# A planned graph-and-experts kernel whose list scheduler gets a finer model, searches its order by small changes, and makes weight loads wait for gathered rows

## The chip, the cores and the metric

The kernel runs on one core of a Trainium2 chip. The metric is device time in microseconds of one execution. A profiled execution gives a trace beside it; its span (first to last recorded instruction) is a little shorter than the time of the same execution. Engines are called by the profile's names: PE (TensorE matmuls), PEld (weight loads of TensorE), DVE (VectorE), ACT (ScalarE), POOL (GpSimd), SP (SyncE, which here issues DMAs). Each engine works off its own queue in order and waits for others by semaphores.

## The reference

Input x has 3327 rows of 256 numbers, the adjacency is 3327 by 3327 of zeros and ones with ones on the diagonal. Two layers follow one another, each with a layernorm ahead and a residual around it:

```
def gnn(x, adj, W, a, gamma, beta):                # H = 4 heads of D = 64
    h = (x @ W).reshape(n, H, D)
    s = einsum('nhd,d->nh', h, a[:D, 0] + a[D:, 0])
    e_row = leaky_relu(s, 0.2)
    e = where(adj[:, None, :] > 0, e_row[:, :, None], -9e15)   # same score for all neighbours of a row
    h_prime = einsum('nhm,mhd->nhd', softmax(e, -1), h).reshape(n, H * D)
    return layernorm(h_prime) * gamma + beta

def ffn(x, gate_w, gate_b, w1, w2, w3):            # 16 experts, 256 -> 512 -> 256
    probs = softmax(x @ gate_w + gate_b)
    top_probs, top_idx = top_k(probs, 2)           # the two weights are divided by their sum
    hidden = silu(x @ w1[e]) * (x @ w2[e])
    return sum over the two experts of weight * (hidden @ w3[e])

x = x + gnn(layernorm(x), adj, ...)
x = x + ffn(layernorm(x), ...)
```

Since a row's score is the same for all its neighbours, the softmax weights of a row are equal, and the aggregation is a product of the zero-one adjacency with h.

## The kernel before

**Stages.** Rows are padded to 3328 = 26 tiles of 128 and cut into seven groups of 4, 4, 4, 4, 3, 4 and 3 tiles. The *h stage* takes a group's rows: statistics on DVE (L503, L504), transposes and the product with W on PE (L484, L492), then a split of the result into a high part (ACT, L495) and a low part (DVE, L498, called lo). Column sums of W that make the scores are worked out ahead of it (L462 to L472). The *aggregation* has 7 x 7 = 49 steps, one for a pair of groups: SP loads a block of the transposed adjacency (L572, sg), DVE converts it (L575, mk), and PE multiplies it with the high and the low part (L598, L599), 676 times each. A *group's end* follows its last step: DVE and POOL make the normalised rows (L653 to L706; square roots on POOL, L435 to L438), PE transposes the result x1 (L722), ACT copies it, and PE makes the gate's logits (L730) and turns them back (L739). DVE finds the two best experts, PE works out each row's place in its expert's list (L784 to L788, L823), ACT writes normed rows (L716), and SP stores them to `normed` in DRAM (L839) and x1 to the output (L614).

**Expert lists.** There are 19 lists of rows. Lists 0 to 2 hold the rows of experts 0 to 2 from the first five groups, lists 3 to 5 the rest of these experts, lists 6 to 18 the other thirteen experts. For a list POOL gathers rows of `normed` by an indirect DMA (L970), one for every 128 rows; DVE picks the row's weight out of the gathered row ("weigh", L976 and L978, which so waits for the DMA); the rows are transposed, for lists below 8 on PE (L1174, ACT copy L1183), from 8 on by DMA transposes of their 16-bit halves (L1137, L1138, L1128). Lists below 6 use plain up products (L985), a silu on ACT (L1198) and a product on DVE (L1201). Lists from 6 on use a scheme with seven products for eight (`by_sevenths`: sums of weights and rows on DVE at L1018, products L1046, copies on ACT L1052 and adds on DVE L1056, silu L1078, product L1081). Down products are L1099 (L1095 for a part of a tile). The result is scaled by the row's weight on ACT (L1222) or DVE (L1224) into the tile y, and POOL adds its rows into the output by an indirect DMA (L1102). SP loads an expert's three weight blocks (L330 to L332) into w12e and w3e; for lists from 6 on it reads the expert's number from a table first.

**What sets the order.** No queue is written by hand. Every piece of work is entered with `plan.add(engine, cost, rank, after, emit, uses, landing, size, slack, step)`. `uses` names buffers with a number of slots each (six for y, three for gathered rows, four for accumulators of the aggregation). `order` is a list scheduler: among all works whose predecessors are placed it takes the one that can start earliest, ties by rank, with a little luck added to works of rank 3. `start_of` works out that earliest start: the engine's free time, predecessors' ends plus HOP (nothing for a predecessor on the same engine), and the freeing of a slot. `place` books it; a DMA with a size goes through one line with a rate, in order of issue. `run` makes 80 orders from 80 seeds, replays each six times with up to 10% noise on the costs of engines other than PE, and emits the instructions in the order with the least total. So every engine's queue is the order of emission, and all costs are only numbers for the planner; an instruction waits for what it really depends on.

Of the kernel before, what the change touches and what calls it, by code (L numbers as in the profile page):

```python
# [37 lines left out]

# [13 lines left out]
ALU = mybir.AluOpType  # L52
# [7 lines left out]
H = 4  # L60
# [55 lines left out]
class Plan:  # L116
# [3 lines left out]
    HOP = 0.2  # L120
    RATE = 380e3
    ORDERS, LUCK = 80, 0.2
    REPLAYS, SPREAD = 6, 0.1
# [13 lines left out]
    def restart(self):  # L137
        for work in self.works:
            work.end = None
        self.free = {work.engine: 0.0 for work in self.works}  # L140
        self.taken, self.held, self.line = {name: [] for name in self.slots}, set(), 0.0

    def start_of(self, work, slack):

        at = self.free[work.engine]
        for w in work.after:
            if w.end is None:
                return None
            at = max(at, w.end + (0 if w.engine == work.engine and not w.landing else self.HOP + slack))
# [11 lines left out]
    def place(self, work, at, cost):  # L161
# [4 lines left out]
        self.free[work.engine] = work.end = at + cost  # L166
# [6 lines left out]
    def order(self, seed):  # L173

        draw = random.Random(seed).random
        luck = {work: draw() * self.LUCK if seed and not callable(work.rank) and work.rank[0] == 3 else 0.0 for work in self.works}
        self.restart()
        todo, order, step = list(self.works), [], -1
        while todo:
            best = None  # L180
            for work in todo:
                at = self.start_of(work, work.slack)
                if at is not None:
                    rank = work.rank(step) if callable(work.rank) else work.rank
                    if best is None or (at + luck[work], rank) < best[:2]:
                        best = (at + luck[work], rank, at, work)
            if best is None:
                return None
            _, _, at, work = best
            todo.remove(work)  # L190
            order.append(work)
            self.place(work, at, work.cost)
            step = step if work.step is None else work.step
# [10 lines left out]

    def run(self):
        orders = [order for order in map(self.order, range(self.ORDERS)) if order]
        order = min(orders, key=lambda o: sum(self.replay(o, seed) for seed in range(1, self.REPLAYS + 1)))
# [11 lines left out]
def gnn_moe(ctx: ExitStack, tc: tile.TileContext, x, adj_t, W, a, gamma, beta, gate_w, gate_b, w1, w2, w3, out):  # L219
# [107 lines left out]
    def load_weights(tiles, e):  # L327

        at = bass.ds(e, 1)
        nc.sync.dma_start(tiles[0], w1[at].rearrange("o (k p) h -> p (o k) h", p=P))  # L330
# [97 lines left out]
    def roots(key, kind, n, out, src, made, rank, uses=(), shifted=True):  # L428
# [12 lines left out]
        s = [plan.add(ACT, 0.69, rank, [m], lambda t=t: nc.scalar.activation(  # L441
            out(t), src(t), AF.Square, bias=mean()[:, t:t + 1], accum_out=T[key]["spread_" + kind][:, t:t + 1]),
            list(uses) + [key]) for t in range(n)]
        return m, plan.add(POOL, 1.4 + 0.3 * shifted, (0,), s, root, [key])
# [29 lines left out]
    def h_stage(g):  # L474
# [37 lines left out]
        for part in ([[t] for t in range(n)] if g == 0 else [list(range(n))]):  # L512
            s = [plan.add(DVE, 0.53, (1, g), [LOADED.get((g, t), LOADED.get(g))], lambda t=t: stats(t), [few]) for t in part]
            r = plan.add(POOL, 1.3, (0,), s, lambda part=part: roots(part[0], part[-1] + 1), [few])
# [3 lines left out]
        for t in range(n):  # L518
            rank = (1, g, t)
            pt, ph, xnt = ("pt", "h", g, t), ("ph", "h", g, t), ("xnt", g, t)  # L520
            w = plan.add(PE, 0.3, rank, [LOADED.get((g, t), LOADED.get(g))], lambda t=t: turn_both(t), [pt])
            read.append(w)
            w = plan.add(ACT, 0.38, rank, [w], lambda t=t: copy_turned(t), [pt, xnt])
            w = plan.add(PE, 0.93, rank, [w] + SCORES, lambda t=t: product(t), [xnt, ph])
            c = plan.add(ACT, 0.38, rank, [w, rooted[t]], lambda t=t: high(t), [ph, few])
            SPLIT[tiles[t]] = plan.add(DVE, 0.42, rank, [c], lambda t=t: low(t), [ph, few])
# [39 lines left out]
    def adjacency(step):  # L566
# [17 lines left out]
        CONVERTED.append(plan.add(DVE, 0.1 + m * n * 0.069, rank, [w] + CONVERTED[-1:], convert, [sk, mk]))  # L584
        return CONVERTED[-1]

    def products(step, masked):
# [16 lines left out]
        for k, (i, t) in enumerate(order):  # L604
            w = plan.add(PE, 0.2405, (2, step, k), [masked, SPLIT[GROUPS[mg][i]]], lambda i=i, t=t: product(i, t),
# [16 lines left out]
    def finish(g, terms, added, tables):  # L622
# [65 lines left out]
        co = plan.add(DVE, 1.6, dve, copies + terms, coefficients, [ak, fk])  # L688
        rests = [plan.add(POOL, 1.2, rank, [co], lambda t=t: rest(t, min(t + 2, n)), [hk, fk]) for t in range(0, n, 2)]
        if swift:  # L690
            scales = [plan.add(DVE, 0.38, dve, [co], lambda t=t: scaled(t), [ak, fk]) for t in range(n)]
        else:
            scales = [plan.add(ACT, 1.34, rank, [co], lambda t=t: scaled_heads(t), [ak, fk]) for t in range(n)]
        hs = [plan.add(DVE, 0.5, dve, [rests[t // 2], scales[t]], lambda t=t: summed(t), [ak, hk, fk]) for t in range(n)]
# [14 lines left out]
        ws = [plan.add(DVE, 0.45, rank, [mean], lambda t=t: centered(t), [ak, hk, fk]) for t in range(n)]  # L709
        x1 = [plan.add(DVE, 0.56, dve, [ws[t], root, added], lambda t=t: rooted(t), [ak, fk]) for t in range(n)]  # L710
# [7 lines left out]
        xn = [plan.add(ACT, 0.55, (3, g + late, 9), [root], lambda t=t: normed_row(t), [pk, fk]) for t in range(n)]  # L718
# [24 lines left out]
        for t in range(n):  # L743
            w = plan.add(PE, 0.3, (0, g), [x1[t]], lambda t=t: turn_both(t), [("pt", g, t)], slack=slack)
# [4 lines left out]
        w = plan.add(PE, 0.1 + 0.08 * n, (0, g), copied + GATE, logits, [xk, gk], slack=slack)  # L749
        w = plan.add(ACT, 0.25, rank, [w], lambda: nc.scalar.copy(some("turned")[:m], psum(gk)[:m, :P]), [gk, fk])  # L750
        gated = [plan.add(PE, 0.16, (0, g), [w], turn_back, [gk, fk], slack=slack)]
# [20 lines left out]
        def gap():  # L772
            return some("gap")
# [52 lines left out]
        w = plan.add(DVE, 0.35, rank, gated + [root], biased, [gk, fk])  # L826
# [584 lines left out]
```

## Time and profile before

| | |
|---|---|
| time, median of 6 | 506.23 us (504.61 to 507.98) |
| profiled execution, its own time | 505.96 us |
| its span | 504.3 us |
| granted TensorE clock | 0.998 |
| instructions | 9541 |
| first matmul, last matmul's end, last issue of an add, end of the span | 1.28, 498.20, 499.41, 504.27 us |
| aggregation ends | about 216 us |
| weights of list 1, 2, 6, 7, 8, 9 issued (L330) | 216.40, 222.37, 263.64, 266.51, 275.57, 282.23 us |
| landing of w12e, least, median, most | 3.7, 5.2, 9.4 us |
| landing of a gather, of an add, median | 4.2, 4.2 us |

The groups of instructions that take most of PE, from the page's table (line, engine, operation, tiles, shapes and number; busy us and mean ns of one; idle time of the engine before them and who ended it):

```profile
L598 PE MATMUL pa<-hi,mk 128*128 128x258 f32 x676 | 167.6, 289 | 0.9 <-DVE mk L575 0.9
L599 PE MATMUL pa<-lo,mk 128*128 128x256 f32 x676 | 163.3, 281 | 0.0
L1099 PE MATMUL ph<-w3e,hid 128*128 128x256 f32 (+5 forms) x400 | 93.9, 379 | 0.0
L1046 PE MATMUL pt<-xt,w12e 128*128 128x256 f32 (+8 forms) x208 | 46.3, 346 | 2.1 <-DVE pa L1056 1.2
```

A mean of 289 ns for one product is not its cost: matmuls overlap in the pipeline, and starts of L598 and L599 follow each other at about 0.12 us. Busy times of a group are unions over such overlaps.

### The profile page before, as it was taken

The numbers are of one execution on the slowest core, as the hardware profiler recorded it, in microseconds if no ns is written. First come the engines' busy times: TensorE is split into PE (matmuls) and PEld (weight loads), VectorE is DVE, ScalarE is ACT, GpSimd is POOL, SyncE is SP. The second block draws the span as 40 slices with busy tenths as digits, with TensorE's granted clock in tenths as the row PEclk, the third lists the DMA queues.
The fourth block names the chain that finished last, engine by engine and source line by source line (L and its number), as shares of the span: only waits on it lengthen the run. The fifth ranks groups of instructions, "written<-read, shape, count | busy, mean of one in ns | idle before, by whom it ended". The sixth has DMA issues, their size and how long they took to land. (4 is left out here: it accounts for less than half of the span.)

```text
span 504.3 us, 9541 instructions
## 1 busy us (share of the span) xinstructions
PE 489.1 (97%) x3239; PEld 443.6 (88%) x3240; DVE 348.9 (69%) x1035; ACT 237.5 (47%) x637; POOL 221.7 (44%) x240
## 2 busy tenths in 40 slices
PE   7999999999999999999999989999999999999995
PEld 4789999999999999976777768999998999988994
DVE  6877654795869879867974459674667678777521
ACT  3453053628164553157321356655556555545442
POOL 5230012212131221457667767846665574543353
PEclk9999999999999999999999999999999999999999
DMA  8942888898878989275339955999888987752243
GB/s 274 350 171 64 291 254 278 283 296 287 243 258 280 364 271 352 80 251 133 101 67 298 335 110 111 212 119 215 145 172 261 223 133 182 177 149 33 33 45 36
DMA packets 85703, 100.06 MB, mean 198 GB/s; under 512 B 27150, under 2 KB 59154, under 8 KB 85652
## 3 DMA queue, kind: packets, MB, share of 16 engines
q1 hardware_dynamic: 74612, 85.42, 55.2%
q0 software_dynamic: 10768, 13.75, 18.0%
q8 instruction: 26, 0.43, 0.4%
q10 hardware_dynamic: 272, 0.26, 0.1%
q14 instruction: 25, 0.20, 0.1%
HBM read 81.55 MB, written 13.75 MB: 189 GB/s over the span
## 5 line engine op out<-in xcount | busy, mean ns | idle before, releaser
L598 PE MATMUL pa<-hi,mk 128*128 128x258 f32 x676 | 167.6, 289 | 0.9 <-DVE mk L575 0.9
L599 PE MATMUL pa<-lo,mk 128*128 128x256 f32 x676 | 163.3, 281 | 0.0
L1102 POOL DMA_INDIRECT out<-y,out_index x61 | 100.4, 1646 | 85.5 <-ACT y L1222 62.4
L598 PEld LDWEIGHTS pa<-hi,mk 128*128 128x128 f32 x676 | 127.7, 189 | 2.2 <-DVE mk L575 1.1
L599 PEld LDWEIGHTS pa<-lo,mk 128*128 128x128 f32 x676 | 127.5, 189 | 0.1
L1099 PE MATMUL ph<-w3e,hid 128*128 128x256 f32 (+5 forms) x400 | 93.9, 379 | 0.0
L1099 PEld LDWEIGHTS ph<-w3e,hid 128*128 128x128 f32 (+5 forms) x400 | 73.7, 187 | 9.5
L970 POOL DMA_INDIRECT x<-normed,index x61 | 66.0, 1081 | 26.0 <-issue 17.9
L575 DVE TENSOR_SCALAR mk<-sg 128x2048 fp32r<-128x2048 f32 (+2 forms) x49 | 54.2, 1106 | 30.4 <-PE pa L599 28.3
L1046 PE MATMUL pt<-xt,w12e 128*128 128x256 f32 (+8 forms) x208 | 46.3, 346 | 2.1 <-DVE pa L1056 1.2
L1078 ACT ACTIVATE s<-pa 128x256 f32<-128x256 f32 (+8 forms) x78 | 27.0, 346 | 43.9 <-PE pa L1046 42.4
L664 POOL TENSOR_TENSOR hp<-csum,c 128x512 f32<-128x512 f32 (+1 forms) x14 | 15.1, 1098 | 65.0 <-DVE c L660 65.0
L1046 PEld LDWEIGHTS pt<-xt,w12e 128*128 128x128 f32 x208 | 36.3, 190 | 7.3 <-PE ph L1099 2.1
L1222 ACT ACTIVATE y<-ph,weight 128x256 f32<-128x256 f32 (+4 forms) x50 | 23.6, 473 | 30.9 <-PE ph L1099 29.3
L1081 DVE TENSOR_TENSOR hid<-s,pa 128x256 f32<-128x256 f32 (+8 forms) x78 | 28.9, 371 | 11.7 <-ACT s L1078 10.7
L1052 ACT COPY pa<-pt 128x512 f32<-128x512 f32 (+8 forms) x52 | 25.0, 498 | 15.7 <-PE pt L1046 14.2
L1056 DVE TENSOR_TENSOR c<-pt,qs 128x512 f32<-128x512 f32 (+8 forms) x26 | 15.5, 594 | 23.4 <-ACT pa L1052 23.4
L492 PE MATMUL ph<-w_sb,xnt 128*128 128x260 f32 x104 | 27.2, 397 | 1.1 <-DVE lo L498 0.9
L985 PE MATMUL pa<-xt,w12e 128*128 128x352 f32 (+3 forms) x128 | 26.8, 359 | 0.9 <-DVE hid L1201 0.9
L1056 DVE TENSOR_TENSOR pa<-pt,qs 128x512 f32<-128x512 f32 (+8 forms) x26 | 15.7, 602 | 17.1 <-PE pt L1046 16.5
L985 PEld LDWEIGHTS pa<-xt,w12e 128*128 128x128 f32 x128 | 19.3, 191 | 6.1 <-DVE hid L1201 1.1
L1046 PE MATMUL pa<-xsum,w12e 128*128 128x256 f32 (+8 forms) x104 | 22.8, 342 | 0.0
(213 smaller groups left out, 821.0 us busy)
## 6 DMA issues: line engine op xcount, KB each, us to landing
sg<-in_adj_t SPq DMA_DIRECT2D x25, 1024.0 KB, 6.0
sg<-in_adj_t SPq DMA_DIRECT2D x20, 768.0 KB, 6.0
w12e<-in_ffn_w SPq DMA_DIRECT2D x30, 512.0 KB, 5.8
w3e<-in_ffn_w SPq DMA_DIRECT2D x15, 512.0 KB, 6.3
normed<-pay SPq DMA_DIRECT2D x5, 520.0 KB, 7.1
out<-x SPq DMA_DIRECT2D x5, 512.0 KB, 5.9
sg<-in_adj_t SPq DMA_DIRECT2D x4, 576.0 KB, 3.8
x<-in_x SPq DMA_DIRECT2D x4, 512.0 KB, 8.4
```

The source lines that it names most:

```text
L492: nc.tensor.matmul(ph[:, :H + D], T["xnt", g, t][:, k, :], w_sb[:, k, :], start=(k == 0), stop=(k == KC - 1))
L575: nc.vector.tensor_scalar(T[mk][:, :m, :n * P], T[sk][:, :m, :n * P], 0.0, None, op0=ALU.is_gt)
L598: nc.tensor.matmul(pa[:, :D + 2], lhs, HI[mg][:, i, H:], start=first, stop=False)
L599: nc.tensor.matmul(pa[:, :D], lhs, LO[mg][:, i, H:], start=False, stop=left[g, t] == 0)
L970: nc.gpsimd.indirect_dma_start(out=xe[:, t, :], out_offset=None, in_=normed[:limit], in_offset=at_rows(idx, t), bounds_check=limit - 1, oo ...
L985: nc.tensor.matmul(p[:, :n], wt[:, k, j * P:(j + 1) * P], xt[:, k, :n], start=(k == 0), stop=(k == KC - 1))
L1046: nc.tensor.matmul(psum(key)[:, w * (CAP // 2):w * (CAP // 2) + half], lhs()[:, w, jp], rhs(), start=first and w == 0, stop=True, skip_gro ...
L1056: return plan.add(DVE, 0.16 + 1.02e-3 * n, (1, i, jp), after, lambda: nc.vector.tensor_tensor(dst(), both(psum(xx)), T[qs][:, :, :half], o ...
L1078: nc.scalar.activation(T[gk][:, t * half:(t + 1) * half], part(0), AF.Silu)
L1081: nc.vector.tensor_mul(T[hk][:, 2 * jp + j, t * half:(t + 1) * half], T[gk][:, t * half:(t + 1) * half], part(1))
L1099: nc.tensor.matmul(py[:m, :D], hid[:, j, t * P:t * P + m], w3e[:, j, :], start=(j == 0), stop=(j == JC - 1))
L1102: i = nc.gpsimd.indirect_dma_start(out=out, out_offset=at_rows(idx, t, m), in_=y[:m], in_offset=None, bounds_check=NP - 1, oob_is_err=Fals ...
```

## The change

Nothing that is computed changes, and no instruction of an engine that computes is added or removed. The planner and its numbers change, and with them the order of the queues; and SP's weight loads get real waits.

The planner's model: HOP falls from 0.2 to 0.04; a new table LAP says how long before (or after) the end of a work its engine is free for the next; DRAIN adds 0.17 to the end of a PE work as others see it; a predecessor on the same engine other than PE now counts with HOP; the rate of the DMA line falls from 380 to 340 KB per us; PE work that follows a rest of over 2.4 us is costed slower for 3.4 us. Instead of 80 random orders, `best_order` makes 40 and then 300 small changes to the best: 3% of the works with luck draw theirs again, and the result is kept if the sum of eight noisy replays is not worse.

```
-    HOP = 0.2
-    RATE = 380e3
-    ORDERS, LUCK = 80, 0.2
-    REPLAYS, SPREAD = 6, 0.1
+    HOP = 0.04
+    LAP = {"PE": 0.0, "ACT": 0.1, "DVE": 0.08, "POOL": -0.31, "SP": -0.05}
+    DRAIN = {"PE": 0.17, "ACT": 0.0, "DVE": 0.0, "POOL": 0.0, "SP": 0.0}
+    RATE = 340e3
+    REST, SLOW = 2.4, 3.4
+    ORDERS, CHANGES, LUCK = 40, 300, 0.2
+    REPLAYS, SPREAD = 8, 0.1
...
-        self.free[work.engine] = work.end = at + cost
+        if work.engine == "PE":
+            if at > self.free["PE"] + self.REST:
+                self.cold = at + self.SLOW
+            cost += min(cost, max(0.0, self.cold - at) / 2)
+        self.free[work.engine] = at + cost - self.LAP[work.engine]
+        work.end = at + cost + self.DRAIN[work.engine]
...
+    def best_order(self):
...
+        best = None
+        for n in range(self.ORDERS + self.CHANGES):
+            luck = {k: draw.random() * self.LUCK for k in lucky} if n < self.ORDERS else {
+                **best[1], **{k: draw.random() * self.LUCK for k in draw.sample(lucky, len(lucky) * 3 // 100)}}
+            order = self.order(luck)
+            if order:
+                end = sum(self.replay(order, seed) for seed in range(1, self.REPLAYS + 1))
+                if best is None or end <= best[0]:
+                    best = (end, luck, order)
+        return best[2]
```

The costs of nearly all works are set anew, mostly by a few hundredths or tenths. Those that go with a new rank, slack, landing or size:

```
-        CONVERTED.append(plan.add(DVE, 0.1 + m * n * 0.069, rank, [w] + CONVERTED[-1:], convert, [sk, mk]))
+        CONVERTED.append(plan.add(DVE, max(0.95, 0.1 + m * n * 0.072), rank, [w] + CONVERTED[-1:], convert, [sk, mk], slack=0.7))
...
-        got = GOT[i] = [plan.add(POOL, 1.33, (1, i), [indexed] + stored, lambda t=t: gather(...), [xek],
-                        landing=2.6) for t, _ in tiles]
+        got = GOT[i] = [plan.add(POOL, 1.08, (1, i), [indexed] + stored, lambda t=t: GATHERED.setdefault(i, []).append(gather(...)), [xek],
+                        landing=1.9, size=150e3) for t, _ in tiles]
...
-        wd = plan.add(DVE, 0.4, (2, i, 9), got, weighed, [xek, ("weight", i)])
+        wd = plan.add(DVE, 0.42, (2, i, 9), got, weighed, [xek, ("weight", i)], slack=6.0)
...
-            ends.append(plan.add(POOL, 1.87, (1, i), [w] + order, lambda t=t, mm=mm, yk=yk: add_rows(
-                T[yk], index_of(i, out_index), t, mm, others, i < EARLY), [yk], landing=2.5))
+            ends.append(plan.add(POOL, 1.64, (4, i), [w] + order, lambda t=t, mm=mm, yk=yk: add_rows(
+                T[yk], index_of(i, out_index), t, mm, others, i < EARLY), [yk], landing=1.5, size=360e3))
...
-    plan.add(PE, 2.2, (0, -1), [], warm_up, [("pt", "warm")])
+    plan.add(PE, 3.9, (0, -1), [], warm_up, [("pt", "warm")])
```

The adds of finished rows so rank behind the gathers on POOL. Slack is counted in `order` only: the scheduler treats such a work as ready that much later than its predecessors' end, and so puts other work of its engine in front of it.

The waits of the weight loads. Before, the planner took a list's gathers as predecessors of the weight loads, but the DMAs did not wait for them; now the first of the three DMAs does:

```
-    def load_weights(tiles, e):
+    def load_weights(tiles, e, behind=()):
         at = bass.ds(e, 1)
-        nc.sync.dma_start(tiles[0], w1[at].rearrange("o (k p) h -> p (o k) h", p=P))
+        first = nc.sync.dma_start(tiles[0], w1[at].rearrange("o (k p) h -> p (o k) h", p=P))
+        for other in behind:
+            tc.add_manual_dep(first.ins, other.ins.name, mybir.DependencyInfo(
+                mybir.DependencyClass.Sync, mybir.DependencyReason.DATA), reason="weights come behind these rows")
...
-    def more_weights(key, source):
+    def more_weights(key, source, behind=None):
         WE[key] = T["w", key]
-        load_weights(WE[key], source())
+        load_weights(WE[key], source(), GATHERED.get(behind, ()))
```

Weights of lists 1 and 2 wait for the gathers of list 0 and 1, those of a list i above 6 for the gathers of list i - 2, those of list 6 for none.

## The prediction

> **What bounds the kernel now.** First the totals, then windows of time, then PE's waits, then what held the engine that each wait names.
>
> ```profile
> PE 489.1 (97%) x3239; PEld 443.6 (88%) x3240; DVE 348.9 (69%) x1035; ACT 237.5 (47%) x637; POOL 221.7 (44%) x240
> ```
>
> TensorE is busy in 97% of the span, so this is a PE-bound program, and no edit here takes a matmul away. Only PE's idle time can be won. Matmul records overlap, so 97% says little about short gaps. The windows say where there are any (columns: PE, weight load, DVE, ACT, POOL busy, granted clock, DMA share, GB/s):
>
> ```profile
> 0.00:20.00 20.00, 17.43 (x83) 12.23 (x85) 14.70 (x52) 7.78 (x20) 9.35 (x59) 1.00 0.86 297
> 40.00:200.00 160.00, 160.00 (x1399) 157.49 (x1398) 119.39 (x389) 71.33 (x244) 29.75 (x35) 1.00 0.84 274
> 260.00:280.00 20.00, 18.91 (x135) 16.40 (x133) 10.35 (x35) 5.11 (x19) 14.98 (x12) 1.00 0.85 253
> 280.00:300.00 20.00, 17.68 (x92) 14.72 (x91) 8.58 (x23) 8.76 (x19) 13.01 (x12) 1.00 0.76 213
> 320.00:480.00 160.00, 160.00 (x879) 147.07 (x878) 108.37 (x255) 88.03 (x191) 87.17 (x62) 1.00 0.77 156
> ```
>
> Two stretches of 160 us, the aggregation and the later expert lists, have no gap: 160.00 of 160.00. Loss sits at the start and between 200 and 320 us, at the change from aggregation to lists. The granted clock is 1.00 in each row, so no gap so far was paid for twice. PE's waits name the gaps:
>
> ```profile
> PE pt L1242 <- DVE neg_half L263: 1.3, 1, 1.3
> PE pt L1046 <- DVE pa L1056: 1.2, 1, 1.2
> PE pa L985 <- DVE hid L1201: 0.9, 1, 0.9
> PE ph L492 <- DVE lo L498: 0.9, 1, 0.9
> PE pa L598 <- DVE mk L575: 0.9, 1, 0.9
> PE pt L1046 <- DVE c L1056: 0.9, 1, 0.9
> PE ph L1099 <- DVE hid L1201: 0.8, 1, 0.8
> PE pt L722 <- ACT xt L1183: 0.6, 1, 0.6
> PE pt L722 <- DVE x L706: 0.5, 2, 0.3
> ```
>
> They are single events, and six of these nine end with DVE, which is busy only half the time there. What held DVE, in its own timeline just before those moments:
>
> ```profile
> 11.10 1.23 DVE L575 TENSOR_SCALAR mk<-sg 128x2048 fp32r<-128x2048 f32 x1 [1.02 <-DMA sg<-in_adj_t]
> 271.03 0.23 DVE L976 SCALAR_TENSOR_TENSOR hit<-x,expert 128x8 f32<-128x8 f32 x1 [2.97 <-DMA x<-normed,index]
> 277.81 0.69 DVE L1018 TENSOR_TENSOR hp<-w12e 128x512 f32<-128x512 f32 x1 [1.87 <-DMA w12e<-in_ffn_w]
> 291.91 0.24 DVE L976 SCALAR_TENSOR_TENSOR hit<-x,expert 128x8 f32<-128x8 f32 x1 [4.41 <-DMA x<-normed,index]
> 300.11 0.23 DVE L976 SCALAR_TENSOR_TENSOR hit<-x,expert 128x8 f32<-128x8 f32 x1 [2.43 <-DMA x<-normed,index]
> ```
>
> The bracket is DVE's idle time and what ended it. DVE's queue is in order: a 0.23 us "weigh" (L976) stands at its head waiting for gathered rows, and the piece of work PE needs stands behind it. So the bound at these places is the order of DVE's queue against DMA landings.
>
> **The change part by part.** All of it is a new order of the same instructions, plus one kind of wait on SP; positions below are those in the queues that the two planners write. Prices are PE time, against the profiled 505.96 us (span 504.3, 1.7 around it; the median of six is 506.23, 0.27 above it).
>
> 1. Start. The first mask conversion goes behind two "lo" (L498) and the next group's first stats. It no longer blocks DVE for 1.02 us on its load at 11 us; a second one does the same at 21.43 (0.99). PE's two waits, 0.9 (L598) and 0.9 (L492), go: −1.8. Against it, the score columns (L462) fall behind one more pair of stats, 0.42 + 0.18 = 0.60 us, and the first h product waits for them: +0.6. Bounds −1.8 to +0.6; the stall at 11 us disappears because 14 to 18 aggregation products stand before the end of the h stage instead of 42. I take −1.2.
> 2. Group 5's end. Its eight transposes (L722) move 30 products (about 30 × 0.24 = 7 us) ahead of the end of aggregation. The 0.5 us for x1 (L706) can be filled by products that remain: −0.5. The 0.6 us on the ACT copy (L1183) belongs to list 0, which has nothing in reserve: kept. Bounds 0 to −1.1.
> 3. Lists 3 to 8. The weigh of list 6 moves from in front of list 3's product (L1201) to behind list 6's row sums, those of 7 and 8 behind L1056 and the halves (L1138); three L1201 of list 5 pass the L1018 that waits 1.87 us for weights. That removes the four list stalls: 0.8 + 0.9 + 1.2 + 0.9 = 3.8. DVE idles over 9 us in the two windows that hold them, so the moved work fits. A weigh that comes later is needed only by the scaled y, tens of us on. Bounds 0 (the next item waits for the same DMA) to −3.8; I take −3.8 and charge what is late next in part 6.
> 4. Weights wait for gathers. Nothing of compute queues behind the waiting SP instruction, only its own next weights, stores and DMA transposes. Weights 1 were issued at 216.40; now the store out<-x (221.94 before) and the gathers of list 0 stand ahead of them, so about 222. Landing is 5.2 us median and 9.4 at most: 227 to 231.4 against first use at 230.57 (L985). Price 0 to +0.9; I take 0, being nearer the median, and the cover is list 0's 8 us of transposes and products. Weights 8 wait for gathers of list 6, which land at about 276 where they were issued at 275.57; weights 9 for list 7's, about 281 against 282.23. Their first readers (L1018) run at 303.7 and 315: 20 us of cover. A gain is possible too, gathers landing earlier without weights beside them, but after part 3 nothing on the path waits for them: 0.
>
> The trace's rows for weights are 5.2 us median landing and uses tens of us later. The Trainium skill, "DMA: Bandwidth & Descriptors", section "Rules for kernel authors", advises to issue a DMA early and to wait late; it speaks against this wait. By the rule the 5 us taken from weights 1 would be lost cover and the sum 0.9 worse; by the landing row nothing is lost.
>
> 5. POOL. Adds of lists 3 to 5 (L1102) fall behind gathers 9 to 12. Each add is 1.65 to 2.0 us, each gather 1.0 to 1.5; the total is unchanged and POOL is 44% busy. Price 0 while y slots last (rival B).
> 6. Late next. A new order has stalls of its own. The nearest rows are the kept ones, 0.2 to 0.6 us. Bounds 0 to +3.8 (each removed list stall replaced by its like); I take +1.0, two of 0.5.
>
> Aggregation in the steady part and lists from 9 on are left at 0: there PE has no idle time to win, and the tail (last product 498.20, last add 499.41, end 504.27) keeps its order.
>
> Sum: −1.2 − 0.5 − 3.8 + 0 + 0 + 1.0 = −4.5. 505.96 − 4.5 = 501.5 on the profiled run's scale, 501.7 against the median.
>
> **Rivals.**
> A. *The stalls move.* DVE passes the weigh and stops at the next instruction for the same rows (halves, L1138) or weights. For it: gathers land late because POOL issues late (list 8's until 288.41 + 4.2), and that stays. Against: L1138 feeds lists 20 us on. The four list stalls return, +3.8, and start and transposes give −1.7, new ones +1.0: −1.7 + 1.0 = −0.7, 505.5.
>
> B. *POOL's adds hold the y buffers; slower.* The tile y has six buffers. The three tiles of lists 3 to 5 used to be added at 277.46, 284.99 and 291.95; now behind gather 12, whose last issue was at 314.72. List 6 scales its four tiles (ACT, L1222) from 314.76 to 320.81, and the fourth needs a freed buffer: an add at 314 to 316, plus 1.65 and a landing of 4.2, frees it at 320 to 322. Then adds 4 and 5 push list 6's adds by some 6 to 9 us, and list 7 scales from 333.06. The margin is between −1 and +4 us. From the point where it is gone, ACT stops in its queue, its copies (L1052) behind, and PE after them. Price: 1 to 4 us in each of lists 6, 7 and 8, say 8. 505.96 − 4.5 + 8 = 509.5. For it: POOL is busy 73% of 260 to 320 us (43.89 of 60). Against: with three adds and their waits (1.41, 1.61, 1.24 us) out of the way, gathers end up to 9 us sooner.
>
> C. *More is won.* All named waits but the first go: 8.9 − 1.3 = 7.6, and some 20 fewer switches between kinds of product at about 0.05 us (start-to-start times of the products exceed each shape's usual one by 33 us in all, 11 of it in gaps over 0.25 us; the other 22 over some 460 runs of one kind) give 1.0; less 0.6 for the score columns: −8.0, 498.2.
>
> **How the numbers follow.** Forecast 0.49, A 0.15, B 0.22, C 0.14. The predicted time is the forecast's, 501.7; its own range is 499.5 to 504. About 0.3% (1.5 us) is the least that can be told from no change. Faster than that (under 504.7): forecast, C and a little of A, 0.64; within: most of A, 0.14; slower: B, 0.22. The range 497.5 to 508 takes in C, A and the smaller half of B.
>
> **What would show it.** Right: no conversion wait by DVE near 11 and 21 us; window 280 to 300 with PE above 19.5; no L976 ahead of a PE wait on L1201 or L1056; PE never waiting for w12e. Wrong: L985 waiting for weights at 230 us (part 4); ACT L1222 idle for a landing of out<-y near 315 to 340 (B); new PE waits on the DVE lines summing to over 3 us (A); or any 160 us window losing its full PE row, which no step above allows for.

## The result and the profile after

| | before | after |
|---|---|---|
| median of the measurement | 506.16 us (504.44 to 509.57, 86 runs) | 505.44 us (502.57 to 507.43, 42 runs) |
| profiled execution, its span | 505.96, 504.3 us | 504.55, 502.9 us |
| PE's last product ends | 498.20 us | 495.16 us |
| last issue of an add | 499.41 us | 498.01 us |

The ratio of the times is 0.9983, with a 95% interval of 0.9974 to 0.9992. Ratios here and below are worked out from fast runs alone and the times given are medians of all runs, so a ratio is not always the quotient of two of them. The change gains 0.7 us of the median and 1.4 us of the profiled execution; 4.5 were forecast. The direction holds. The time lies in the wide range (497.5 to 508) but above the forecast's own one (499.5 to 504). The size is wrong, and the gain lies inside the 1.5 us that the prediction counts as no change. The profiled execution of after is 0.9 us below the median of its 42 runs, that of before 0.2 below its own. What follows is read from this one pair, and so shares out 1.4 us.

The page's first part, for after:

```profile
PE 490.2 (97%) x3239; PEld 445.2 (89%) x3240; DVE 350.3 (70%) x1035; ACT 236.6 (47%) x637; POOL 221.8 (44%) x240
```

That says nothing: the same work in a span 1.4 us shorter. Windows of after tell more (PE is the second number; before had 18.91, 17.68 and 18.20 in these three):

```profile
260.00:280.00 20.00, 19.75 (x141) 17.36 (x140) 9.71 (x36) 5.59 (x20) 11.54 (x12) 1.00 0.75 228
280.00:300.00 20.00, 19.76 (x102) 16.40 (x101) 14.37 (x36) 10.89 (x22) 14.43 (x13) 1.00 0.81 242
...
480.00:500.00 20.00, 15.05 (x84) 12.92 (x82) 4.43 (x12) 6.44 (x17) 10.85 (x7) 0.97 0.37 42
```

The stretch of the early lists is nearly full now, as forecast. The last row is low because PE is done at 495.16. PE's waits in after, the largest three:

```profile
PE pt L759 <- DVE x L743: 1.6, 1, 1.6
PE pt L1279 <- DVE neg_half L297: 1.3, 1, 1.3
PE pt L759 <- ACT xt L783: 0.5, 1, 0.5
```

(After's lines are before's plus about 37: L759 is before's L722, L743 is L706, L1022 is L985, L1083 is L1046, L1136 is L1099, L1139 is L1102, L1259 is L1222.) Of the nine waits shown for before, the warm-up's 1.3 stays and the conversions, the "lo", and all four stalls of the lists are gone. One new wait of 1.6 us stands at group 5's end.

Short gaps don't show in such a table. For a balance, take for each product the time from its start to the next start, and count its difference from the usual value of its line and shape (the 30th percentile over both profiles). Where PE loses time, in us:

| stretch (us) | before | after | difference |
|---|---|---|---|
| 0 to 40, start | 6.0 | 5.1 | -0.9 |
| 40 to 210, aggregation | 7.1 | 7.75 | +0.65 |
| 210 to 230, group 5's end | 3.05 | 4.2 | +1.15 |
| 230 to 310, lists 1 to 7 | 8.75 | 3.95 | -4.8 |
| 310 to the end of PE | 4.3 | 5.2 | +0.9 |
| sum | 29.2 | 26.2 | -3.0 |

The split is good to some 0.2 us: with products grouped by line and shape in a slightly different way the differences come out at -0.9, +0.65, +1.1, -4.6 and +0.7, again -3.0 in all. So PE won 3.0 us. The span won 1.4. The other 1.6 went between PE's last product and the end. The timeline of the last adds, first before's (start, length, engine, line, idle time before it and what ended it):

```profile
480.54 1.62 POOL L1102 DMA_INDIRECT out<-y,out_index  x1 [0.30 <-issue]
485.16 1.57 POOL L1102 DMA_INDIRECT out<-y,out_index  x1 [3.01 <-DMA out<-y,out_index]
...
488.89 1.62 POOL L1102 DMA_INDIRECT out<-y,out_index  x1 [0.30 <-ACT qs L1052]
494.78 0.47 ACT L1222 ACTIVATE y<-ph,weight 128x256 f32<-128x256 f32 x1 [1.36 <-PE ph L1099]
495.66 1.57 POOL L1102 DMA_INDIRECT out<-y,out_index  x1 [5.14 <-ACT y L1222]
```

and after's:

```profile
479.88 1.62 POOL L1139 DMA_INDIRECT out<-y,out_index  x1 [1.34 <-ACT y L1259]
484.53 1.57 POOL L1139 DMA_INDIRECT out<-y,out_index  x1 [3.03 <-DMA out<-y,out_index]
...
488.29 1.61 POOL L1139 DMA_INDIRECT out<-y,out_index  x1 [0.30 <-ACT s L1115]
491.74 0.47 ACT L1259 ACTIVATE y<-ph,weight 128x256 f32<-128x256 f32 x1 [1.36 <-PE ph L1136]
494.26 1.58 POOL L1139 DMA_INDIRECT out<-y,out_index  x1 [4.36 <-ACT y L1259]
```

Before, list 18's first add goes 0.88 us after its y starts (494.78 to 495.66): the y was what it waited for. After, it goes 2.52 us after (491.74 to 494.26). The bracket names ACT's y, but that had ended at 492.21. What was late is the landing of list 17's adds, which list 18's must wait for. So the end hangs on a chain: the third add of list 16 at 479.88, then 4.65 us until list 17's first (the bracket at 484.53 names the landing), 3.76 to its third, 5.97 to list 18's first. That first link was issued at 480.54 in before. It came only 0.66 us earlier, though PE was 3.4 us ahead by then: after's PE queue puts the down products of a tile of list 17, and two products of list 18, in front of list 16's last tile.

Group 5's end is the other place. Timelines of POOL, DVE and ACT there, after:

```profile
200.76 2.88 POOL L701 TENSOR_TENSOR hp<-csum,c 128x512 f32<-128x512 f32 x2 [12.52 <-DVE c L697]
201.46 2.45 DVE L707 TENSOR_TENSOR agg<-agg,c 128x256 f32<-128x256 f32 x2
204.18 0.75 DVE L707 TENSOR_TENSOR agg<-agg,c 128x256 f32<-128x256 f32 x2
...
208.35 1.51 POOL L1007 DMA_INDIRECT x<-normed,index  x1 [4.72 <-issue]
209.05 0.19 ACT L478 ACTIVATION_READ_ACCUMULATOR unused<-hp,mean_hp 128x1 f32 x1
210.17 1.44 POOL L1007 DMA_INDIRECT x<-normed,index  x1 [0.30 <-issue]
211.68 0.19 POOL L472 TENSOR_SCALAR rs_hp<-spread_hp 128x4 f32<-128x4 f32 x1
211.95 1.04 POOL L473 TENSOR_TENSOR rs_hp<-rs_hp,neg_half 128x4 f32<-128x4 f32 x1
213.02 0.48 DVE L743 SCALAR_TENSOR_TENSOR x<-agg,rs_hp,x 128x256 f32<-128x256 f32 x1 [1.90 <-POOL rs_hp L473]
```

Two of DVE's scalings take 2.45 us while POOL multiplies beside them and 0.75 alone. ACT's last sum for the square root ends at 209.24, but POOL's root (L472, L473) stands behind two gathers (1.51 and 1.44 us from 208.35 on) and starts at 211.68. So x1 starts at 213.02 and PE's transposes at 213.57, while PE had started the last product in front of them at 211.73. No run here takes the scalings' or the gathers' delay away, so what each of the two is worth isn't shown.

### The profile page after: what moved, and what is told of

Same layout as the page of the kernel before. It is cut to its first block, busy times and chain, and to the rows that moved or that the text cites. A ratio compares the mean times of both kernels' runs of the same rounds, so it can differ in the third digit from the quotient of the medians.

```text
span 502.9 us, 9593 instructions
## 1 busy us (share of the span) xinstructions
PE 490.2 (97%) x3239; PEld 445.2 (89%) x3240; DVE 350.3 (70%) x1035; ACT 236.6 (47%) x637; POOL 221.8 (44%) x240
## 4 chain that ended last, share of the span: by engine, by line
PE 86%; DVE 6%; issue 3%; DMA 1%; POOL 1%; ACT 1%; POOLq 1%; SPq 0%; DVEq 0%; ACTq 0%
PE ph L1136 17%; PE pa L1083 15%; PE pa L635 13%; PE pa L636 12%; PE pt L1083 11%; PE pa L1022 6%; PE ph L529 5%; PE pt L521 1%; PE pt L759 1%; DVE mk L612 1%; PE ph L1132 1%; PE ph L767 1%; PE ph L860 1%; DMA out<-y,out_index 1%; DVE agg L707 1%
## 5 line engine op out<-in xcount | busy, mean ns | idle before, releaser
L1139 POOL DMA_INDIRECT out<-y,out_index x61 | 98.2, 1610 | 89.8 <-ACT y L1259 63.6
L1136 PE MATMUL ph<-w3e,hid 128*128 128x256 f32 (+5 forms) x400 | 91.4, 380 | 0.0
L1136 PEld LDWEIGHTS ph<-w3e,hid 128*128 128x128 f32 (+5 forms) x400 | 73.9, 187 | 10.4 <-issue 0.2
L701 POOL TENSOR_TENSOR hp<-csum,c 128x512 f32<-128x512 f32 (+1 forms) x14 | 16.5, 1199 | 73.4 <-DVE c L697 58.4
L1083 PE MATMUL pt<-xt,w12e 128*128 128x256 f32 (+8 forms) x208 | 45.8, 345 | 0.1
L1259 ACT ACTIVATE y<-ph,weight 128x256 f32<-128x256 f32 (+4 forms) x50 | 23.6, 472 | 43.0 <-PE ph L1136 39.0
L1083 PEld LDWEIGHTS pt<-xt,w12e 128*128 128x128 f32 x208 | 36.2, 190 | 4.3 <-PE ph L1136 2.1
L1022 PE MATMUL pa<-xt,w12e 128*128 128x352 f32 (+3 forms) x128 | 26.4, 358 | 0.0
L1022 PEld LDWEIGHTS pa<-xt,w12e 128*128 128x128 f32 x128 | 19.2, 191 | 5.0 <-issue 0.6
L715 ACT ACTIVATE agg<-agg,c 128x64 f32<-128x64 f32 x76 | 18.9, 336 | 9.7 <-DVE c L697 5.3
```

What stands on the lines that cost most here:

```text
L1022: nc.tensor.matmul(p[:, :n], wt[:, k, j * P:(j + 1) * P], xt[:, k, :n], start=(k == 0), stop=(k == KC - 1))
L1083: nc.tensor.matmul(psum(key)[:, w * (CAP // 2):w * (CAP // 2) + half], lhs()[:, w, jp], rhs(), start=first and w == 0, stop=True, skip_gro ...
L1136: nc.tensor.matmul(py[:m, :D], hid[:, j, t * P:t * P + m], w3e[:, j, :], start=(j == 0), stop=(j == JC - 1))
L1139: i = nc.gpsimd.indirect_dma_start(out=out, out_offset=at_rows(idx, t, m), in_=y[:m], in_offset=None, bounds_check=NP - 1, oob_is_err=Fals ...
```

## The experiments

All experiments ran after the main measurement, on four chips on which before takes 512 to 514 us instead of 506: e1 to e4 on the first, e5 to e8 on the second, e9 to e12 on the third, e13 to e16 on the fourth. Each ratio is to runs of before on the same chip. These runs show a disturbance that the main measurement doesn't, which e9 and e12 to e15 are about. It is put down to the chips here; that it came with something else that had changed since isn't ruled out. Where an order is held, a list of the plan's works replaces the search, so that nothing but the named edit moves.

**e1, e8: after's own order, held.**

```
-        order = self.best_order()
+        order = [self.works[k] for k in ORDER]
```

> The changed kernel's queues, held fixed as a list; a second profile and a second timing of the same program. Theory (the gain is real on PE, 3.0 us, and half is lost behind the last product): last product ends 494.5 to 496.0, end of the span 7.5 to 8.0 us behind it, ratio to before 0.998 (0.997 to 0.999). Rival (the profiled execution was a lucky one and PE gains less on average): last product after 496.5.

> The changed kernel's queues again. If the 1.1% loss of e1 belongs to that chip alone: ratio to before 0.997 to 0.9995. If the first timing was the exception: over 1.005 again, with a stretch of half clock near 280 us.

e1: 520.31 us, ratio 1.011 [1.0075, 1.0146]. e8: 519.4 us, 1.0101 [1.0062, 1.014]. The same instructions that take 0.998 of before in the main measurement are 1% slower than before here. e1's windows:

```profile
270.00:280.00 10.00, 7.11 (x46) 5.82 (x45) 1.31 (x5) 1.33 (x5) 6.85 (x7) 0.95 0.99 320
280.00:290.00 10.00, 8.17 (x50) 6.93 (x50) 5.54 (x14) 1.76 (x7) 6.35 (x6) 0.88 0.64 209
```

PE is idle in a stretch that was full in the main profile (19.75 of 20 from 260 to 280), and the clock falls to 0.95 and 0.88 behind it.

**e2: weights don't wait for gathers.**

```
-        load_weights(WE[key], source(), GATHERED.get(behind, ()))
+        load_weights(WE[key], source(), ())
```

> The same queues, the first weight DMA waits for no gathers. Theory (the waits are covered): ratio to e1_held 0.999 to 1.001, first up product of list 1 not later. Rival 1 (weights crowd the gathers, the waits win something): gathers of lists 6 to 8 land later, DVE waits for x again near 280 to 300 us, +1 to +3 us. Rival 2 (the waits cost): -0.5 to -1.5 us.

518.87 us, 1.0124 [1.008, 1.0169], beside e1's 1.011. No gain and no loss that can be measured.

**e3, e16: the tail mended.** List 16's last tile goes in front of list 17, list 18's first two products behind list 17's downs. The move in PE's queue (operation, tiles, width of the product, number in a row; ACT's copies move along):

```
-L1136 Matmult ph<-w3e,hid 128x256 x10
+L1136 Matmult ph<-w3e,hid 128x256 x6
+L1136 Matmult ph<-w3e,hid 120x256 x4
+L1136 Matmult ph<-w3e,hid 128x256 x8
+L1136 Matmult ph<-w3e,hid 120x256 x4
 L1083 Matmult pt<-xt,w12e 128x168 x2
 L1083 Matmult pa<-agg,hp 128x168 x2
-L1136 Matmult ph<-w3e,hid 120x256 x4
-L1136 Matmult ph<-w3e,hid 128x256 x4
-L1136 Matmult ph<-w3e,hid 120x256 x4
```

> PE and ACT finish list 16's third tile before list 17's first one, and the first two products of list 18 come after list 17. Theory (adds of a list wait until those of the list before have landed, so list 16's late tile sets the end): list 16's last add goes 2.3 to 2.9 us sooner, list 18's first add 0.3 to 0.6 us after its y, span 1.2 to 1.8 us shorter at the same end of PE; ratio to e1_held 0.9965 to 0.998. Rival (something else holds POOL's queue before the last three adds): the last add unmoved, span within 0.4.

> The kernel of e3 (after with the tail mended) once more, beside the same runs of before, to see whether a chip on which before takes 506 us gives it the 1.6 us of the tail: there 503.8, ratio 0.995; on a chip where before takes 512 to 514, as in e3, 518 to 520 and a loss of 8 us between 270 and 290 us.

e3: 519.53 us, 1.0125 [1.0085, 1.0165]. e16: 515.64 us, 1.0068 [1.0029, 1.0107]. Times here spread over several us, so 1.6 can't be read from e3's. Its timeline shows it:

```profile
506.95 0.48 ACT L1259 ACTIVATE y<-ph,weight 128x256 f32<-128x256 f32 x1 [1.36 <-PE ph L1136]
507.83 1.58 POOL L1139 DMA_INDIRECT out<-y,out_index  x1 [5.56 <-ACT y L1259]
```

and e1's, with after's tail, on the same chip:

```profile
508.24 0.47 ACT L1259 ACTIVATE y<-ph,weight 128x256 f32<-128x256 f32 x1 [1.36 <-PE ph L1136]
510.74 1.57 POOL L1139 DMA_INDIRECT out<-y,out_index  x1 [4.33 <-ACT y L1259]
```

The first add follows its y by 0.88 us again in e3, and from that y to the end of the span it is 9.35 us, where e1 takes 11.06. The chain is what held the end, and 1.6 to 1.7 us is its price. It is after's order that makes it: in all six profiles with after's tail (after, e1, e2, e4, e8, e9) the add comes 2.50 to 2.59 us after the start of y, in those with before's or the mended one 0.75 to 0.88. In e16 PE loses 5.9 us between 270 and 290, where 8 were expected, and the time is under the 518 to 520 expected for such a chip.

**e4, e7: group 5's transposes later** (e7 with the tail mended too). Eight more pairs of products stand in front of them:

```
+L635 Matmult pa<-hi_151,mk 128x258
+L636 Matmult pa<-lo_158,mk 128x256
...
 L759 Matmult pt<-ident,x_63 128x128 x4
```

> The first four of group 5's transposes of x1 go behind 8 more aggregation products, the other four follow two products later. Theory (they stand in front of x1): the 1.6 us wait of PE for DVE's x at 212 us goes, PE is 1.3 to 1.6 us ahead from there to its end, ratio to e1_held 0.997 to 0.9985. Rival (the gate or list 0 then waits for the copies instead): PE's wait for ACT's turned x1 grows by over 0.8 us, total within 0.4 us.

> The changed kernel with the tail of e3 and group 5's transposes of e4. Theory: on a chip like the first one the 1.6 us wait at 212 us goes and list 18's first add follows its y by under 0.7 us; 2.5 to 3.3 us below e8, ratio to before 0.991 to 0.994. Rival (one of both is taken back elsewhere): 0 to 1.8 us below e8.

e4: 517.87 us, 1.008 [1.0055, 1.0104]. e7: 516.59 us, 1.0074 [1.0041, 1.0108]. The wait of 1.6 us is gone from both profiles, but the gate's product waits in its place (0.8 us, "PE ph L767 <- ACT xt L783"), as do transposes of list 0 (0.8). By the same balance the edit wins some 0.3 to 0.6 us between 200 and 230 (e4 and e7 against the profiles in the held order), not 1.6. What is late is x1 itself, and more products in front mostly move the place where PE waits for it.

**e5, e6: before, and before with only DVE's queue changed.** In e6 the weigh of lists 6 to 8 and their halves move behind the work they held up, and list 5's products (L1201) pass the sums that wait for weights:

```
-L1201 TensorTensor hid<-s,pa 128x88
-L976 TensorScalarPtr hit<-x_58,expert 128x8
-L978 TensorReduce weight<-hit 128x4
-L1201 TensorTensor hid<-s,pa 128x88 x2
+L1201 TensorTensor hid<-s,pa 128x88 x3
...
 L1018 TensorTensor xsum<-xt,agg 128x256
+L976 TensorScalarPtr hit<-x_58,expert 128x8
+L978 TensorReduce weight<-hit 128x4
```

> The kernel before, for its profile beside the others on the same chip. On a chip like that of e1 to e4 (513.6 us): PE behind by over 5 us of its own first profile, with waits at the same lines and somewhere a stretch of half clock. On a chip like the first one: last product 497.5 to 499.

> The kernel before, with DVE's queue alone changed: the weigh of lists 6 to 9 moved behind the work that PE waits for, and three L1201 of list 5 ahead of list 7's L1018, as in the changed kernel. Theory (part 3 of the prediction holds): PE's four waits of 0.8 to 1.2 us at 270 to 301 us go, the last product 3.0 to 4.0 us earlier and, as before's tail is kept, the whole 3.0 to 4.0 us shorter: ratio 0.992 to 0.994. Rival (DVE stops at the next instruction for the same rows): ratio 0.998 to 1.0.

e5: 513.22 us. e6: 514.53 us, 1.0002 [0.9968, 1.0036]. The four stalls aimed at don't occur in e6. PE's waits there:

```profile
PE pt L1046 <- DVE pa L1056: 4.6, 1, 4.6
PE pa L994 <- DVE y L1224: 2.0, 1, 2.0
```

One of 4.6 us at 313 and one of 2.0 at 281 us stand in their place. The same waits in e5, with nothing moved:

```profile
PE pa L1046 <- ACT pa L1052: 3.9, 1, 3.9
PE pt L1046 <- DVE pa L1056: 3.0, 1, 3.0
PE pt L1046 <- DVE c L1056: 0.8, 1, 0.8
```

Of the four stalls, PE's wait for list 5's product at 281 us doesn't occur in e5 either, the one before it is 0.4 us instead of 0.8 and not put down to DVE, one has grown from 1.2 to 3.0, and one is as it was. So e6 is no clean test of part 3: the 3.8 us as forecast are not there to be won. By the balance e5 loses 4.1 us between 303 and 320, where the first profile of before loses nothing, and e6 8.2. Part of e6's loss is the chip's disturbance; the profiles don't tell whether the edit adds to it.

**e9, e12: adds back between the gathers** (e12 with the tail mended). In after's POOL queue twelve gathers of lists 6 to 8 and sixteen of lists 9 to 12 stand in a row, with two adds of list 2 between and those of lists 3 to 5 behind. Here the adds stand between the gathers of lists 6 to 9:

```
 L1007 DMACopy x_58<-normed,index_101 128x260 x4
-L1007 DMACopy x_59<-normed,index_101 128x260 x4
-L1007 DMACopy x_63<-normed,index_101 128x260 x4
 L1139 DMACopy out<-y,out_index_102 3328x256 x2
...
+L1007 DMACopy x_59<-normed,index_101 128x260 x3
+L1139 DMACopy out<-y,out_index_103 3328x256
+L1007 DMACopy x_59<-normed,index_101 128x260
+L1007 DMACopy x_63<-normed,index_101 128x260 x2
+L1139 DMACopy out<-y,out_index_103 3328x256
...
-L1139 DMACopy out<-y,out_index_103 3328x256 x2
```

> The changed kernel's queues, with POOL's adds of lists 2 to 5 back between the gathers of lists 6 to 9, as before the change. Theory (the adds' place costs nothing, part 5 of the prediction): within 0.3% of e1 and e8. Rival (on the slower chip the uninterrupted run of eight gathers at 268 to 278 us goes with the late completions of PE there): PE's losses between 270 and 290 us shrink by 3 us or more and no half clock near 280 us.

> e9's POOL queue with e3's tail. Theory: list 18's first add 0.9 us behind the start of its y, 1.6 us below e9. Rival: the tail's gain is lost again, within 0.5 us of e9.

e9: 520.35 us, 1.0114 [1.0008, 1.022]. e12: 514.36 us, 1.0056 [1.0005, 1.0106]. PE's loss between 270 and 290 falls from 8.4 us (e8) to 3.0, and the granted clock stays at 1.00 from 270 to 290 (e8 has 0.90 and 0.76 in the two halves of it). But it comes back between 310 and 320 us (about 8 in e9, 6.3 in e12), where the next unbroken run of gathers is, 15 in a row from 297 to 317 in e12. e8 ran on another chip than e9 and e12; e16, e13 and e14, which share one, lose 5.9 us between 270 and 290 with after's places of the adds and 3.1 with the adds between.

**e10, e11: the search and the model apart.** e10 is after with 80 random orders instead of the search; e11 is before's model and costs with the new search.

```
-    ORDERS, CHANGES, LUCK = 40, 300, 0.2
+    ORDERS, CHANGES, LUCK = 80, 0, 0.2
```

> The changed kernel with the old search: 80 random orders and no small changes; model, costs and weight waits as changed. Its plan ends 2 to 3 us later by the planner's own count. Theory (the model brings the order, the search little): within 0.3% of e8, same tail. Rival (the search brings the gain): 0.4 to 0.8% above e8.

> The kernel before with the new search alone: 40 random orders and 300 small changes, eight replays; model, costs and weights' DMAs as before. Theory (a search in a model that is off by several us finds orders that are better only in the model): ratio to before 0.997 to 1.004. Rival (the search is worth it by itself): 0.990 to 0.996.

e10: 520.31 us, 1.0143 [1.0068, 1.0219]. e11: 515.84 us, 1.0065 [1.0035, 1.0096]. Neither half is faster than before on this chip, and e11 is slower than both of its forecasts. What each is worth in the main measurement stays open. The late tail comes with what e10 keeps of the change (model, costs, ranks, waits) and not with the search: list 18's first add comes 2.67 us after the start of its y in e10, 0.87 in e11.

**e13, e14, e15: are the gathers the disturbance?** All three are e12 with an edit to the gathers of lists 9 to 12: left out, replaced by plain loads from POOL, or spaced by memsets.

```
+    def plain(xe, idx, t, limit=NP):
+        return nc.gpsimd.dma_start(xe[:, t, :], normed[t * P:(t + 1) * P])
...
+    def spaced(xe, idx, t, limit=NP):
+        for _ in range(3):
+            nc.gpsimd.memset(idle, 0.0)
+        return gather(xe, idx, t, limit)
```

> The kernel of e12 (adds between the gathers, tail mended) with the gathers of lists 9 to 12 left out, so that these lists work on the rows of lists 6 to 9 and their sums are wrong; everything else is issued as in e12, except that the weights of lists 11 to 14 have no gathers to wait for. Theory G (an unbroken run of gathers on POOL makes PE's completions late): the start-to-start loss of PE from 300 to 330 us, 6.3 us in e12, falls to 2 or less, no stretch of half clock near 315, span some 4 to 6 us below e12's 512.7. Rival P (PE's own load, the density of the products of by_sevenths, makes the completions late): loss and half clock stay within 1 us of e12's.

> The kernel of e12 with the gathers of lists 9 to 12 replaced by plain loads of as many rows that follow one another, issued by POOL in the same places, so that these lists work on other rows. The same bytes move. If it is the writing of 128 descriptors by POOL for each gather that disturbs PE, the loss from 300 to 330 us falls as in e13 (2 or less). If it is the bytes or their landing, or PE itself, it stays near 6.

> The kernel of e12 with three small memsets of a scratch tile on POOL ahead of each gather of lists 9 to 12, so that a gather follows the one before by some 2.2 instead of 1.31 us; POOL idles for 9.9 us behind the run in e12, so nothing waits for it. Nothing computed changes. Theory G, if the density of the run matters: loss from 300 to 330 us down to 3 to 4, time 2 to 3 us below e12's 514.4. If any gather costs its share, whatever the distance: the same loss spread over a longer time, time as e12 within 1 us.

First e12's timeline at 309 us, to see what the loss is:

```profile
309.93 1.03 PE L1136 MATMUL ph<-w3e,hid 128*128 128x256 f32 x4
313.11 0.70 DVE L1093 TENSOR_TENSOR pa<-pt,qs 128x512 f32<-128x512 f32 x1 [3.81 <-remote]
313.87 1.54 PE L1083 MATMUL pt<-xt,w12e 128*128 128x256 f32 x4 [2.91 <-issue]
315.27 0.38 ACT L1115 ACTIVATE s<-pa 128x256 f32<-128x256 f32 x1 [5.19 <-remote]
```

PE has issued everything up to 310.58 (four groups from 307.23 on). DVE waits for a group whose last product started at 308.85, and gets it at 313.11; ACT waits behind, then PE. "Remote" is a semaphore event that the trace ties to no instruction. The events of PE's own semaphore stand at 304.15, 306.40, 307.13 and then 313.09: the products' completions reached DVE late, by some 4 us, while POOL's gathers went on at their 1.31 us. The wait of DVE is what shows this. The list of events alone wouldn't, for events are missing in it: e12's trace holds 481 for the 539 instructions of PE that update this semaphore, and of DVE's and ACT's 731 of 808 and 439 of 497, while after's holds all. (They are missing in e13 too, 497 of 536, without the loss.) Whether the products ended late or the news of it came late isn't shown. The window from 300 to 330 us in e12, e13 and e14:

```profile
300.00:330.00 30.00, 25.81 (x111) 21.57 (x110) 19.87 (x44) 15.85 (x29) 15.84 (x16) 0.94 0.61 144
```

```profile
300.00:330.00 30.00, 30.00 (x143) 26.66 (x142) 24.14 (x55) 20.31 (x38) 6.14 (x6) 1.00 0.57 123
```

```profile
300.00:330.00 30.00, 27.24 (x127) 23.52 (x126) 21.29 (x49) 18.11 (x34) 11.43 (x17) 1.00 0.94 166
```

Without the gathers PE is busy in all 30 us at full clock, and its loss from 300 to 360 us is 0.2 us instead of 7.5; PE ends 7.0 us earlier (499.72 instead of 506.74). With plain loads the loss is 3.5: about half. PE's queue is the same in all three, so its own load alone doesn't make the loss, and the gathers are what was taken away. Two things weaken this. e12 ran on another chip than e13 and e14; on theirs e16, with all its gathers, lost 4.7 us from 300 to 360. And e14's profiled execution (511.47 us) is the slowest of its ten, so that plain loads leave half of the loss holds for that execution only. The times: e13 510.99 us, 0.9967 [0.9927, 1.0008]; e14 507.97 us, 0.9945 [0.991, 0.9979]; e15 525.1 us, 1.0283 [1.0188, 1.0378]. e13's span gains only 3.4 of the 7.0 us: 7.1 us pass there from the end of the last add's record to the end of the span, against 3.3 in e12, in which no engine computes; why is open.

e15 doesn't tell what it was made for. Its expectation took it that nothing waits for the gathers, and that was wrong. At 2.5 to 3.0 us apart they come late, and a copy of rows stands at the head of ACT's queue until they land (timeline of e15, whose L1180 is L1174 of after):

```profile
329.01 1.05 ACT L1180 COPY halves<-x 128x1024 uint16<-128x1024 uint16 x1 [9.29 <-DMA x<-normed,index]
```

It waits 9.29 us there and 5.04 for the list before, ACT's y and copies stand behind it, and PE waits 6.1 and 3.6 us for these. That is rival A's mechanism, an in-order queue with an early instruction at its head, brought about by the edit. Whether the distance of gathers matters for PE's completions stays open.

The Trainium skill, "DMA: Bandwidth & Descriptors", section "SWDGE vs HWDGE vs iDMA", says that POOL writes the descriptors of its DMAs itself, into rings in SBUF, and that this path, unlike SP's, can be disturbed by DVE in its two-port mode. What suffers there is POOL's writing of descriptors. In e12 the gathers kept their pace, and it was PE's completions that came late to DVE.

## Why the prediction was wrong, point by point

Two steps failed, each by 1.6 to 1.65 us: the tail, which was left at 0, and group 5's end.

*Start (part 1, -1.2):* measured -0.9. Right. No conversion stands ahead of a PE wait any more.

*Steady aggregation (left at 0):* +0.65. A wait of 0.5 us of L759 on an ACT copy at 111 us is new. The prediction named "any 160 us window losing its full PE row" as a sign against it, and the row from 40 to 200 us fell from 160.00 to 159.49.

*Group 5's end (part 2, -0.5):* +1.15, the wrong sign. The step took it that "the 0.5 us for x1 (L706) can be filled by products that remain". Thirty products do remain, but behind the transposes in PE's queue, and x1 comes 1.56 us later than PE runs out of those in front. (Their 7 us are counted twice: the 0.24 us are those of a pair, since starts follow each other at 0.12, so thirty products are 3.6 us.) The prediction priced the cover, not the thing covered: the scalings at 2.45 instead of 0.75 us, and the root behind two gathers. The numbers were there: before's trace has three such scalings in 2.39 us beside POOL and one in 0.41 alone. e4 and e7 show that more cover in front wins some 0.6 us at most. That these two delays make x1 late is read from the timeline; no run removes them.

*Lists (parts 3 and 6, -3.8 and +1.0):* -4.8 from 230 to 310 us, and +0.9 later. The four named stalls are gone from the main profile and less came in their place there than was charged. That DVE's new order alone does it isn't shown: e6 changed it alone, on a chip where two of the four stalls are smaller or gone even in before and the disturbance hides a gain of that size.

*Weights that wait (part 4, 0):* right. Weights of list 1 were issued at 219.75 us (about 222 was said), list 1's products at 231.59 don't wait for them, and e2 shows no difference.

*POOL's adds (part 5, 0; rival B):* the y buffers did run short, at list 7 (ACT in after's profile):

```profile
336.67 0.47 ACT L1259 ACTIVATE y<-ph,weight 128x256 f32<-128x256 f32 x1 [3.41 <-DMA out<-y,out_index]
```

ACT stands for 3.41 us until an add of an earlier list has landed, and for 0.59 at 338.67. That is rival B's mechanism and the sign that the prediction gave for it. Its price hardly fell due: PE had down products in its queue until 335 and lost some 0.3 us between 330 and 340, a part of the +0.9, where B asked 1 to 4 us in each of three lists. So part 5's 0 was nearly right in size, and the margin was used up.

*The tail:* this step failed, and with the plainest cause. The prediction left the stretch from list 9 on at 0, since "the tail (last product 498.20, last add 499.41, end 504.27) keeps its order", and took each us of PE for a us of time. The tail's order did change, in PE's queue, by one tile and two products, and there the end belongs to a second resource: the chain of adds, each list's waiting for the landing of the list's before. In before it had little slack: list 18's y came at 494.78, 5.9 us after the third add of list 17 was issued, and that add's own successor could go 5.97 us after it (after's value). So it would have taken over after a gain of under 1 us, unless the adds of list 16 moved up too. Of PE's 3.0 us the chain took 1.64; e3's timeline, with these moved back, gives them back, and so do those of e7, e12 and e16. On the chip of the main measurement this wasn't tried; 504.55 - 1.64 = 502.9 is an estimate for the profiled run there.

The sum by steps: -0.9 + 0.65 + 1.15 - 4.8 + 0.9 = -3.0 for PE, + 1.64 for the tail = -1.4. Of the 3.1 us between -4.5 and -1.4, the tail is 1.6, group 5 1.65, the aggregation 0.65 and the start 0.3; the lists gave 1.0 more than part 3 asked, and the 0.9 lost from 310 us on stands for the 1.0 that part 6 charged.

*Readings:* the prediction says that six of its nine waits end with DVE; eight do. Its sums for the forecast and rival B stand on the profiled run's scale, those for A and C on the median's, 0.27 us above. Neither changes the account.

Rival A gave 505.5 for "the stalls move" and is nearest to the measured time by number, but not by its mechanism: the stalls of the lists did not move. The gain was taken by the end.

## What to carry to other kernels

When an engine is busy for 97% of a span, the time it wins counts only as far as the next resource at the end has slack. Follow the last transfers back to the first link of their chain and compare the links with the engine's own end, before adding gains up. When cover is put in front of a late result, price the result's own chain on its engines, at the durations they show side by side and not alone.

A difference of a few tenths of a per cent between two orders of the same instructions may not hold in other runs on another chip: after's order was 0.998 of before in the main measurement and 1.010 to 1.011 on two others.

## What was not expected of the hardware

*Completions of PE that come late in runs of gathers.* In e12 DVE got a group of PE's products some 4 us late, in a run of POOL's gathers, and with 16 gathers left out, on another chip, PE's loss from 300 to 360 us was 0.2 instead of 7.5 us (e13). Profiles on all four chips have losses of this kind. In the main profile after's gathers, at the same pitch of 1.31 us, left PE undisturbed:

```profile
300.00:330.00 30.00, 30.00 (x144) 27.05 (x144) 23.21 (x50) 20.00 (x38) 18.60 (x16) 1.00 0.88 167
```

What differs between these chips the traces don't show, apart from the missing events.

*Two engines side by side.* DVE's scalings of 128x256 took 1.2 us each beside POOL's products and 0.38 each alone. The Trainium skill, "GPSIMD Engine Reference", section "8. Key points", states that POOL shares its SBUF interfaces with DVE's instructions that read two inputs from SBUF; the rows agree in that, and the factor here is 3.3 (2.45 against 0.75).

*The clock behind a stall.* In e1 the granted clock was 0.95 and 0.88 in the two windows with PE's stalls from 272 us on, and 1.00 in the window before. In the main profiles it stays at 1.00 in all windows shown up to 320 us.
